# Two small vectors made in the prologue, and attention's last window inverted ahead of its predecessor's division

## The chip, the cores and the metric

The kernel runs on one core of one Trainium2 chip. The metric is the device time of one execution in microseconds (us), the median of several runs. A profile is one further execution, recorded by the hardware profiler. The engines of the core appear in it as PE (TensorE, the matrix multiplications), PEld (its weight loads), DVE (VectorE), ACT (ScalarE), POOL (GpSimd) and SP (SyncE, which issues most DMA transfers).

## The reference

Two layers work on an image batch `x` of shape (2, 56, 56, 384), all in fp32. Cut to what is computed:

```python
# layer 0: neighbourhood attention (12 heads of 32, 7x7 keys), then an MLP
q, k, v = split(layer_norm(x) @ w_qkv + b_qkv)
attn = softmax(q * 32**-0.5 @ k_nb + rpb)          # 49 neighbours of each position
x = x + (attn @ v_nb) @ w_proj + b_proj
x = x + gelu(layer_norm(x) @ w1 + b1) @ w2 + b2
# layer 1: convolution with four decaying scans, then an MLP
p = layer_norm(x) @ w_in + b_in                    # 384 -> 768
local = depthwise_conv3x3(p)
mixed = 0.25 * (lr + rl + tb + bt)(local) + local  # scans along rows and columns
mixed = layer_norm(mixed) * on_g + on_b
x = x + mixed @ w_out + b_out                      # 768 -> 384
x = x + gelu(layer_norm(x) @ w1 + b1) @ w2 + b2
```

The norm ahead of `w_out` is folded into the weights by the kernel. It needs two sums over the 768 rows of `w_out`: one weighted with `on_b`, which is added to the bias, and one weighted with `on_g / 768`, which is taken off every row. The two vectors of weights, side by side, are the tile `pair`.

## The kernel before, in words

**Order of work.** Each engine runs its own list of instructions in the order in which the kernel issues them; semaphores hold an instruction back until what it needs is there. The order is written out by hand. The stages are: a prologue (to about 50 us), attention (to about 661 us), the MLP of layer 0 over groups of 512 tokens with `w_in` of layer 1 behind it and the convolution beside it, and the MLP of layer 1.

**Prologue.** The constants go into a pool `const` first: `zeros` (line 191), `ident`, `chan` (all per-channel vectors, among them `on_g` and `on_b`, fetched by one DMA). The first group of tokens is normalised on VectorE and turned on TensorE. Then VectorE makes `bq` (line 691), the scaled bias of the queries, and takes the statistics of the second group (line 218).

**Attention.** The image is cut into 56 windows of 8x14 queries. For each window TensorE makes scores (line 539), VectorE adds the position bias (L550), ScalarE exponentiates (L560), and TensorE sums values (L579) and denominators (L590). Iteration `t` of a loop works on one part of the stream; a window is finished in three steps, which VectorE and GpSimd share:

- `gather` (L500, L505): VectorE transposes the sums into `turned`, and GpSimd copies one column of it into `totals`;
- `invert` (L509, L513 twice, L515): VectorE takes the reciprocal and checks that the totals are within bounds, and GpSimd spreads the reciprocals over `wide`;
- `divide` (L519, L522): VectorE transposes `wide` into `rec_t` and multiplies the attention output `og` by it.

`wide` has one buffer, and `turned` and `rec_t` share one. In iteration `t`, the window gathered in the iteration before is inverted at the top, and divided near the end. After the last part, `t == NS`, only the gathering of the last window is left; its inversion is at the top of `t == NS + 1`. TensorE then projects the last tokens (L609), which GpSimd prepares by adding the residual to the bias (L603).

**MLP with convolution beside it.** A group's MLP has 12 hidden blocks of 128 channels (`hidden`: three matmuls on L1185 and a GELU on ScalarE, L1196), then four products with `w2` (L1203), evicted by VectorE into the sum with the input (L1846), with statistics (L218, L219) after each. Products alternate between two PSUM banks, `y` and `y_end`. A planner, `Beside`, puts the convolution's steps on VectorE between these: taps (L1281), scans (L1228, L1232) and their sum (L1297). It deals out steps by fixed costs while the kernel is built.

**The sums of `w_out`.** In the fifth group of layer 0, a generator `prepare_w_out` is advanced once ahead of each hidden block. Its first step makes `pair` on VectorE (L1131, L1132) and takes the bank `y_end`; each of the next six issues one matmul (L1136) with a slice of `pair` as the stationary operand; then VectorE copies the two sums (L1142), they go through DRAM to all partitions (L1143, L1145), and `w_out` is rewritten (L1150, L1152). On TensorE the order is: three matmuls of block 0, L1136, three of block 1, L1136, and so on.

## Time and profile before

| what | value |
|---|---|
| median of 3 runs (lowest, highest) | 2602.36 us (2600.61, 2603.96) |
| the profiled execution's own time | 2603.72 us |
| its span, first to last instruction | 2601.9 us |
| PE busy | 2571.9 us, 99% |
| DVE busy | 1963.4 us, 75% |
| ACT busy | 982.2 us, 38% |
| POOL busy | 466.7 us, 18% |
| mean granted clock of TensorE | 0.997 |
| `pair` (L1131, L1132), one each | 0.164 and 0.161 us, at 912.6 us |
| `rec` (L509) x56, median | 0.218 us |
| `rec_t` (L519) x56, median | 0.571 us |
| `wide` on POOL (L515) x56, median | 0.534 us |

Busy time is the time in which an engine worked on an instruction, not a measure of how well. The list of waits says for each engine what it stood idle for, in total, how often and how long at most; the releaser is inferred from the semaphores. Timelines give the start from the beginning of the span and the duration; neighbouring instructions of one line are merged (xN), and a bracket shows idle time before them with its releaser. Each fp32 matmul of the program leaves two records. In the table by stretch, the columns are the length, the busy time of PE, PEld, DVE, ACT and POOL with the number of instructions, the granted clock of TensorE (1.00 is full speed), the busy share of the DMA engines, and GB/s.

### The profile page before, as it was taken

How to read it: one execution, taken by the hardware profiler on the slowest of the kernel's cores; microseconds unless marked ns; L12 is line 12 of the kernel's file. 1: busy time of each engine (PE TensorE's matmuls, PEld its weight loads, DVE VectorE, ACT ScalarE, POOL GpSimd, SP SyncE). 2: the span in 40 equal slices, each digit the busy share in tenths (PEclk: the TensorE clock that was granted, in tenths of full speed). 3: DMA queues.
4: the chain of work that ended last, by engine and by line, in shares of the span. 5: the costliest groups of instructions: out<-in, count | busy, mean ns of one | idle time of the engine just before them, and what ended most of it. 6: DMA issues, size and time to landing. Idle time of an engine off the chain costs nothing. (4 is left out here: it accounts for less than half of the span.)

```text
span 2601.9 us, 39993 instructions
## 1 busy us (share of the span) xinstructions
PE 2571.9 (99%) x16146; PEld 1643.9 (63%) x16148; DVE 1963.4 (75%) x3481; ACT 982.2 (38%) x1748; POOL 466.7 (18%) x457
## 2 busy tenths in 40 slices
PE   9999999999999999999999999999999999999999
PEld 5666666666798545555445555555555557888888
DVE  4888878887344378688998889889988836888871
ACT  5655555654443232223344423212233312333222
POOL 0111212111652000000010000000010042444342
PEclk9999999999999999999999999999999999999999
DMA  7423454225301232233346534533254331111000
GB/s 229 153 83 100 156 193 141 84 95 191 115 31 37 71 115 84 96 119 108 122 151 231 206 112 175 183 121 124 98 213 178 134 103 46 49 49 49 22 13 18
DMA packets 131652, 299.17 MB, mean 115 GB/s; under 512 B 10390, under 2 KB 85760, under 8 KB 129152
## 3 DMA queue, kind: packets, MB, share of 16 engines
q1 hardware_dynamic: 126512, 269.76, 29.9%
q10 hardware_dynamic: 4944, 26.74, 3.0%
q8 instruction: 129, 2.11, 0.3%
q14 instruction: 67, 0.55, 0.1%
HBM read 180.86 MB, written 115.61 MB: 114 GB/s over the span
## 5 line engine op out<-in xcount | busy, mean ns | idle before, releaser
L1185 PE MATMUL mm<-hT,w 128*128 128x512 f32 x1080 | 474.5, 594 | 0.1
L1281 DVE SCALAR_TENSOR_TENSOR loc<-pt,taps,loc 128x990 f32<-128x990 f32 (+9 forms) x336 | 377.2, 1123 | 11.3 <-ACT loc L1263 2.9
L1185 PEld LDWEIGHTS mm<-hT,w 128*128 128x128 f32 x1080 | 202.2, 190 | 240.2 <-issue 233.2
L226 POOL TENSOR_TENSOR rs<-rs,mhalf 128x4 f32<-128x4 f32 (+4 forms) x72 | 89.4, 1242 | 1276.7 <-DVE rs L223 1268.2
L1196 ACT ACTIVATE hid<-mm,chan 128x512 f32<-128x512 f32 x180 | 123.2, 685 | 414.1 <-PE mm L1185 414.1
L1203 PE MATMUL y<-w,hid 128*128 128x384 f32 x792 | 260.9, 486 | 0.0
L1203 PE MATMUL y_end<-w,hid 128*128 128x384 f32 x792 | 260.8, 486 | 0.0
L550 DVE TENSOR_TENSOR pts<-sc,bias 119x448 f32<-119x448 f32 (+5 forms) x396 | 219.3, 616 | 45.7 <-PE sc L539 45.3
L560 ACT ACTIVATE pts<-pts 119x448 f32<-119x448 f32 (+5 forms) x396 | 210.8, 572 | 111.1 <-DVE pts L550 106.1
L1203 PEld LDWEIGHTS y_end<-w,hid 128*128 128x128 f32 x792 | 149.9, 190 | 102.8
L1203 PEld LDWEIGHTS y<-w,hid 128*128 128x128 f32 x792 | 149.8, 190 | 102.8 <-issue 0.5
L393 PE MATMUL ps<-hT,wqkv 128*128 128x448 f32 x504 | 204.8, 550 | 2.1 <-ACT vs L438 1.5
L1185 PE MATMUL mm<-hT,w_in 128*128 128x512 f32 x396 | 172.0, 593 | 1.5 <-DVE hid_u L1571 0.9
L393 PEld LDWEIGHTS ps<-hT,wqkv 128*128 128x128 f32 x504 | 91.3, 189 | 84.4 <-issue 74.2
L1185 PEld LDWEIGHTS mm<-hT,w_in 128*128 128x128 f32 x396 | 75.0, 190 | 96.2 <-issue 91.9
L1168 DVE STREAM_TRANSPOSE hT<-xn 32x96 f32<-32x96 f32 x464 | 124.9, 269 | 11.6 <-ACT xn L244 5.6
L244 ACT ACTIVATE xn<-xc,sh,rs 128x384 f32<-128x384 f32 x98 | 64.4, 699 | 168.6 <-DVE sh L237 168.5
L1414 DVE STREAM_TRANSPOSE turned<-mx 32x192 f32<-32x192 f32 x336 | 123.9, 369 | 4.4
L579 PE MATMUL o<-pts,vt 100*32 100x112 f32 (+3 forms) x3168 | 117.1, 265 | 2.0 <-ACT pts L560 2.0
L539 PEld LDWEIGHTS sc<-qT,kT 32*100 32x100 f32 (+3 forms) x3168 | 87.8, 169 | 46.3 <-DVE sum L569 7.6
L539 PE MATMUL sc<-qT,kT 32*100 32x112 f32 (+3 forms) x3168 | 106.5, 268 | 3.1 <-DVE pts L550 3.1
L609 PE MATMUL ps<-wproj,og 128*128 128x384 f32 x294 | 105.7, 499 | 2.8 <-DVE og L522 2.2
(180 smaller groups left out, 4142.8 us busy)
## 6 DMA issues: line engine op xcount, KB each, us to landing
loc<-loc_d SPq DMA_DIRECT2D x24, 784.0 KB
mixed<-mix_d SPq DMA_DIRECT2D x24, 784.0 KB
mix_d<-mixed SPq DMA_DIRECT2D x24, 784.0 KB
xa<-x_d SPq DMA_DIRECT2D x24, 768.0 KB
bias<-in_bias_t ACTq DMA_DIRECT2D x13, 1344.0 KB
p_d<-mx SPq DMA_DIRECT2D x11, 1536.0 KB
mx<-mix_d SPq DMA_DIRECT2D x11, 1536.0 KB
pt<-p_d SPq DMA_DIRECT2D x18, 560.0 KB
```

Of the source, the lines that this page charges most:

```text
L393: nc.tensor.matmul(ps, lhsT=wqkv[:, c, m * P : (m + 1) * P], rhs=hT[:, c, half_of(n)], start=c == 0, stop=c == NC - 1,)
L539: nc.tensor.matmul(sc[i // 2][: w.keys, i % 2, q : q + TT], lhsT=kT[d, hg, w.keys_at + r * w.kc : w.keys_at + (r + w.rows) * w.kc], rhs=qT ...
L550: nc.vector.tensor_tensor(self.pts[:n, h : h + 2, lo:hi, :], sc[half][:n, :, at * TT : (at + hi - lo) * TT].rearrange("p h (c q) -> p h c ...
L560: nc.scalar.activation(t, t, AF.Exp)
L579: nc.tensor.matmul(o[i * HD : (i + 1) * HD, self.slot, :TT], lhsT=w.vt[:n, c, h * HD : (h + 1) * HD], rhs=self.pts[:n, i, c, :], start=c = ...
L609: nc.tensor.matmul(ps, lhsT=ogs[t // 7][:, c, at : at + P], rhs=wproj[:, c, :], start=c == 0, stop=c == NC - 1,)
L1168: nc.vector.transpose(hT[j : j + HD, :, k * P + i : k * P + i + HD], xn[i : i + HD, k, :].rearrange("p (c q) -> p c q", c=NC)[:, :, j : j ...
L1185: nc.tensor.matmul(ps[:, : n * P], lhsT=w[:, c, m * P : (m + 1) * P], rhs=hT[:, c, : n * P], start=c == 0, stop=c == NC - 1,)
L1196: nc.scalar.activation(t[:, : n * P], ps[:, : n * P], AF.Gelu, bias=col(b1, m))
L1203: nc.tensor.matmul(ps, lhsT=t[:, k * P : (k + 1) * P], rhs=w[:, m, :], start=m == 0, stop=m == len(lhs) - 1,)
L1281: nc.vector.scalar_tensor_tensor(to, pt[:, lo + dy - self.top : hi + dy - self.top, xt : xt + n], self.tap(dy, dx), to, ALU.mult, ALU.add,)
L1414: nc.vector.transpose(t[j : j + HD].rearrange("p (m c) -> p m c", m=NI)[:, :, i : i + HD], mx[i : i + HD, :, k * P + j : k * P + j + HD],)
```

## The change

There are two edits. `pair` moves from the MLP's pool into `const`, and is filled in the prologue, just before `bq`, by two multiplications with a number (one of them 1.0, where a copy was); the two instructions at the start of `prepare_w_out` go. The generator's steps stay as many, and L1136 reads the same values. And the last window is inverted in iteration `NS`, right after it was gathered and ahead of its predecessor's division, instead of at the top of `NS + 1`; the predecessor itself is still inverted at the top of `NS`.

```diff
     zeros = const.tile([P, MT], mybir.dt.bfloat16, name="zeros")
     nc.vector.memset(zeros, 0.0)
+    pair = const.tile([P, NI, 2], F32, name="pair")
     ident = const.tile([P, P], F32, name="ident")
...
         take_x(0, c, tps[c])
+    for i, (name, scale) in enumerate((("L1_conv_on_b", 1.0), ("L1_conv_on_g", 1.0 / INNER))):
+        nc.vector.tensor_scalar_mul(pair[:, :, i], chan[:, COL[name] : COL[name] + NI], scale)
     nc.vector.tensor_scalar_mul(bq, chan[:, COL["b_qk"] : COL["b_qk"] + NC], HD ** -0.5)
...
         store_all("v")
-        if gathered is not None:
+        if gathered is not None and t <= NS:
             gathered.invert()
         inverted, gathered = gathered, None
...
             if hi == units[s].m:
                 units[s].gathered()
+        if t == NS and gathered is not None:
+            gathered.invert()
         if inverted is not None:
             inverted.divide()
...
-            pair = wp.tile([P, NI, 2], F32, name="pair")
-            on = chan[:, COL["L1_conv_on_b"] : COL["L1_conv_on_b"] + NI]
-            og = chan[:, COL["L1_conv_on_g"] : COL["L1_conv_on_g"] + NI]
-            nc.vector.tensor_copy(pair[:, :, 0], on)
-            nc.vector.tensor_scalar_mul(pair[:, :, 1], og, 1.0 / INNER)
             ps = bank()
```

## The prediction

> **What bounds the kernel now.** I read the page first: engine shares and the clock row.

> ```profile
> PE 2571.9 (99%) x16146; PEld 1643.9 (63%) x16148; DVE 1963.4 (75%) x3481; ACT 982.2 (38%) x1748; POOL 466.7 (18%) x457
> ...
> PEclk9999999999999999999999999999999999999999
> ```

> TensorE (PE) is busy for 2571.9 of 2601.9 us, so only its 30 us of idle time, or time at a lower clock, can be saved by edits that remove no matmul. The list of waits of PE, longest first in total, says which idle time the edits touch:

> ```profile
> PE y_end L1136 <- DVE pair L1132: 4.1, 1, 4.1
> ...
> PE ps L609 <- DVE og L522: 2.2, 1, 2.2
> ```

> The first is one wait of 4.1 us, the longest of all, and it is for `pair`; the second is one wait of 2.2 us for attention's last division. Both edits therefore aim at something that TensorE really waits for. Next the timeline around the first (start us, us, engine, line, what):

> ```profile
> 899.74 6.66 DVE L1281 SCALAR_TENSOR_TENSOR loc<-pt,taps,loc 128x1045 f32<-128x1045 f32 x5
> 905.99 2.74 PE L1185 MATMUL mm<-hT,w 128*128 128x512 f32 x6
> 910.21 2.37 DVE L1232 TENSOR_TENSOR_SCAN both<-decay,both 128x1064 f32<-128x1064 f32 x1
> 912.56 0.16 DVE L1131 COPY pair<-chan 128x6 f32<-128x6 f32 x1
> 912.63 0.16 DVE L1132 TENSOR_SCALAR pair<-chan 128x6 f32<-128x6 f32 x1
> 912.84 1.44 PE L1136 MATMUL y_end<-w_out,pair 128*2 128x384 f32 x2 [4.11 <-DVE pair L1132]
> 914.22 3.73 PE L1185 MATMUL mm<-hT,w 128*128 128x512 f32 x6
> 917.88 0.81 PE L1136 MATMUL y_end<-w_out,pair 128*2 128x384 f32 x2
> 918.62 2.84 PE L1185 MATMUL mm<-hT,w 128*128 128x512 f32 x6
> 921.39 0.81 PE L1136 MATMUL y_end<-w_out,pair 128*2 128x384 f32 x2
> ```

> VectorE (DVE) runs a band of the convolution without a pause from 899.74 on, so the two tiny `pair` instructions, which need nothing but constants, come to their turn at 912.56. TensorE finished the first hidden block (L1185) at 908.73 and waits. The first L1136 and the next L1185 are also longer than their successors (1.44 and 3.73 us against 0.81 and 2.84). The busy time by stretch explains it; the column after POOL is the granted clock:

> ```profile
> 909.00:913.00 4.00, 0.16 (x1) 0.09 (x2) 3.93 (x7) 1.52 (x2) 0.28 (x1) 0.95 0.95 339
> 913.00:915.00 2.00, 2.00 (x3) 0.50 (x2) 1.09 (x3) 0.00 (x0) 1.83 (x1) 0.50 0.12 47
> 915.00:918.00 3.00, 3.00 (x7) 0.99 (x6) 2.93 (x4) 0.01 (x1) 0.00 (x0) 0.83 0.37 150
> ```

> After the pause the clock is 0.50, then 0.83 on average: the stall is paid a second time. Last, the timeline at the end of attention:

> ```profile
> 657.92 0.58 DVE L519 STREAM_TRANSPOSE rec_t<-wide 128x384 f32<-128x384 f32 x1 [0.29 <-POOL totals L505]
> 658.60 0.51 DVE L522 TENSOR_TENSOR og<-og,rec_t 128x336 f32<-128x336 f32 x1
> 659.02 0.22 DVE L509 RECIPROCAL rec<-totals 128x12 f32<-128x12 f32 x1
> 659.38 0.51 POOL L515 COPY wide<-rec 128x384 f32<-128x384 f32 x1 [1.49 <-DVE good L513]
> 659.92 0.58 DVE L519 STREAM_TRANSPOSE rec_t<-wide 128x384 f32<-128x384 f32 x1 [0.44 <-POOL wide L515]
> 661.26 0.59 PE L609 MATMUL ps<-wproj,og 128*128 128x384 f32 x1 [2.15 <-DVE og L522]
> ```

> The last window's reciprocal (L509) stands behind its predecessor's division (L519, L522), and TensorE waits for the end of that row.

> [...]

> **The change part by part.** Without the wait, TensorE keeps the rhythm of the later blocks: L1185 to L1136 takes 921.39-918.62 = 2.77, L1136 to L1185 0.74, a period of 3.51 us. From 905.99 the first L1136 would start at 908.76 and the second at 905.99+2.77+3.51 = 912.27, not at 917.88. That is 5.61 us: 4.08 of pause and 1.53 of slow clock (912.84 to 917.88 is 5.04, against 3.51).

> L1136 then waits only for `w_out`'s transfer, issued at 671, and for its bank `y_end`, which VectorE evicted at 898.45 to 899.01. Does something else stop the faster TensorE? ScalarE needs the shift of the norm (L237, until 915.02, unmoved) ahead of its GELU of the third block; that block ends at 905.99+2.74+2*3.51 = 915.75, so the GELU is not late, and there are three banks. VectorE's copy of the sums (L1142) waited 4.5 us for the last L1136 and now finds it done (932.72-5.61 = 927.1) when VectorE gets there, at 928.27: VectorE wins about 4.5 us as well, so the lines queued behind it (the L1120 and the next scan) and the sums' DMAs behind L1143 on SP's queue move along. The difference of 1.1 us is absorbed at the next evictions, where VectorE waits for TensorE; list of VectorE's waits from 933 to 1100:

> ```profile
> DVE xc L1846 <- PE y L1203: 27.2, 4, 16.2
> ```

> From 933 to the end TensorE waits 3.4 us in all (1.6 for L1440, 1.2 for xsums, 0.6 for hT), and each of those producers is itself paced by TensorE or by VectorE. So I keep the whole 5.61. The two removed instructions hold VectorE for 0.07 us each (912.56, 912.63, 912.70): nothing on the path.

> In the prologue two instructions of that kind, also some 0.07 us apart, go in front of `bq` at 8.46. `bq` is first read at 28.99, and VectorE idles 8.12 us before its next instruction (16.75), which waits for a transfer. Cost 0. If that cover were gone it would be 0.15 us. They wait for `chan`, which had landed by 5.80.

> The division: no instruction is added, the reciprocal and the two checks (L509, L513 twice) go in front of L519 and L522 of the predecessor. Reciprocal at 657.92 instead of 659.02; the checks follow at 0.14, the predecessor's L519 another 0.23 later (the spacing at 646.35 to 646.58), at 658.29, ending at 658.87. `wide` has one buffer, so GpSimd's copy may overwrite it only then, not right after the reciprocal: 658.92 to 659.01, against 659.38. Its 0.51 us now run beside the predecessor's L522 (658.97 to 659.48). The last L519 writes the buffer that this L522 reads, so it starts at about 659.58 with the 0.10 us seen from 658.50 to 658.60, against 659.92: 0.34 us, passed on to TensorE at 661.26 and to GpSimd's queue behind the copy (four L603, the norm's L226, the w1 sums), which moves as a whole. Ends: 0 (the order of waits eats it) to 0.5. I take 0.35.

> Sum: 5.61+0.35+0 = 5.96. The profiled execution took 2603.72 us (its span and 1.8 around it) and would take 2597.8; it stood 1.36 over the median of 2602.36. Forecast: 2602.36-5.96 = 2596.4 us, 0.23% less. About 0.2%, 5.2 us, is what a measurement of this kernel can tell from no change, so this forecast lies barely past it.

> **The rivals.** *The pause alone is won.* [...] the trace is one execution; where a typical one pays less at half rate, the gain is 4.08+0.35 = 4.4, giving 2598.0, no change by the bound. For it: one window at 0.50 is all that I have. [...]

> *The wait moves.* The GELU behind L237, the sums' bank or a DMA stops TensorE after all, and a part of the 5.61, 3 us or more, is lost again: 2599.4 to 2602.4. Against it are the margins above, of which ScalarE's, 0.7 us on the GELU and then three banks, is the smallest.

> *The division does nothing*: `wide`'s one buffer holds the copy back until no time is won; 2596.7, inside the main case.

> *Slower.* `pair` now lies in the constants' pool ahead of all attention tiles, which in the built program start 64 bytes later. [...] Priced: 0.2 us in each of attention's 56 windows is 11.2 us, 2602.4-6.0+11.2 = 2607.6; from 0.106 us a window the gain is gone, from 0.2 the kernel is slower beyond the bound. For it: ScalarE, TensorE's feeder, waits for transfers 7.8 us in all between 60 and 661 us, GpSimd 10.1. Against: those are waits for a store's end and for `xr`, none of TensorE's, ScalarE's or VectorE's is for `vt`, which is asked for two windows (some 22 us) ahead, and the DMA engines are 0.39 to 0.44 busy there.

> **How the numbers follow.** Whole gain 0.68 (own range 2594.2 to 2597.6, nine tenths of it past the bound); pause alone 0.16 (a small part past the bound); the wait moves 0.09; slower 0.07. Faster: 0.61+0.02 = 0.63; slower 0.07; the rest, 0.30, within 0.2%. The range leaves out the slower case, most of the moved wait and a tail below: 2593.8 to 2600.2.

> **What would show it.** Right: the wait of L1136 for `pair` is gone from the list; L1136 follows the first L1185 block at once, blocks 3.5 us apart from the first on; the clock is 1.00 from 905 to 920; L1142 no longer waits 4.5 us; L609 waits about 1.8 us instead of 2.15; the copy to `wide` starts right after the predecessor's L519. Wrong: a new wait of TensorE of over 1 us between 905 and 1100, L1136 held by a transfer, or a changed mean of L550 or L560.

## The result and the profile after

| what | before | after |
|---|---|---|
| median, 22 runs of each beside one another (lowest, highest) | 2602.72 us (2598.81, 2607.53) | 2598.77 us (2593.85, 2603.30) |
| ratio to before, 95% interval | | 0.9985 [0.9978, 0.9991] |
| the profiled execution's own time | 2603.72 us | 2598.40 us |
| its span | 2601.9 us | 2596.6 us |
| mean granted clock of TensorE | 0.997 | 0.998 |

The changed kernel takes 3.95 us less (1.5 parts in a thousand; from the interval, 2.3 to 5.7 us). The forecast was 5.96 us less. The time lies in the range, and the sign is right, but by the bound of 0.2% this measurement says "no change" where the likeliest case said "faster". A second measurement of the same kernel, in another set of runs (below), gave 0.9971 [0.9961, 0.9981], that is 7.25 us less by the medians. The forecast ratio, 0.9977, lies between the two.

Lines after 192 stand one line lower in the changed kernel, up to the new loop at 692 (L509 is L510, L522 is L523, L609 is L610); L1136, L1142 and L1185 have kept their numbers. First the page of the changed kernel, engine shares and clock row:

```profile
PE 2570.7 (99%) x16146; PEld 1644.1 (63%) x16148; DVE 1964.2 (76%) x3481; ACT 982.9 (38%) x1748; POOL 467.0 (18%) x457
...
PEclk9999999999999999999999999999999999999999
```

TensorE's busy time is 1.2 us smaller, though it does the same matmuls, which fits less time at half rate (before, the clock was 0.50 from 912.62 to 916.04 us; around the same work it is 1.00 now). The rest of the 5.3 us between the two spans, 4.1 us, is idle time. The waits of PE in the changed kernel, longest first in total (total us, times, longest):

```profile
PE sc L540 <- DVE pts L551: 3.5, 7, 0.7
PE ps L610 <- DVE og L523: 2.1, 1, 2.1
```

The wait for `pair`, 4.1 us and first in the list before, is gone. The wait for the last division is not: 2.12 us, against 2.15. Next the timeline around the first L1136 of the changed kernel (start us, us, engine, line, what):

```profile
906.84 2.74 PE L1185 MATMUL mm<-hT,w 128*128 128x512 f32 x6
909.51 0.81 PE L1136 MATMUL y_end<-w_out,pair 128*2 128x384 f32 x2
910.25 2.84 PE L1185 MATMUL mm<-hT,w 128*128 128x512 f32 x6
913.02 0.81 PE L1136 MATMUL y_end<-w_out,pair 128*2 128x384 f32 x2
...
915.84 0.71 ACT L245 ACTIVATE xn<-xc,sh,rs 128x384 f32<-128x384 f32 x1 [2.03 <-DVE sh L238]
...
928.96 0.54 DVE L1142 COPY sums<-y_end 2x384 f32<-2x384 f32 x1
```

The rhythm is that of the forecast from the first block on: L1136 starts 2.67 us after the block, the next one 3.51 us later, and both take 0.81 us. L1142 has no wait in front of it, where VectorE stood idle for 4.49 us before. ScalarE waits 2.03 us for the shift of the norm, until 915.84, while TensorE works through its third block and the next L1136 (916.53 in the same timeline) without a stop. The busy time by stretch (length, PE, PEld, DVE, ACT, POOL, clock, DMA share, GB/s), changed kernel:

```profile
909.00:913.00 4.00, 4.00 (x10) 1.14 (x8) 3.93 (x3) 1.76 (x2) 0.00 (x0) 1.00 1.02 339
913.00:915.00 2.00, 2.00 (x6) 0.76 (x6) 1.74 (x3) 0.69 (x1) 1.43 (x1) 1.00 0.26 105
```

TensorE is busy throughout, at the full clock. The last view is the end of attention in the changed kernel:

```profile
658.97 0.23 DVE L510 RECIPROCAL rec<-totals 128x12 f32<-128x12 f32 x1 [0.30 <-POOL totals L506]
659.35 0.57 DVE L520 STREAM_TRANSPOSE rec_t<-wide 128x384 f32<-128x384 f32 x1
660.02 0.51 DVE L523 TENSOR_TENSOR og<-og,rec_t 128x336 f32<-128x336 f32 x1
660.05 0.85 POOL L516 COPY wide<-rec 128x384 f32<-128x384 f32 x1 [1.11 <-DVE rec_t L520]
660.93 0.58 DVE L520 STREAM_TRANSPOSE rec_t<-wide 128x384 f32<-128x384 f32 x1 [0.40 <-POOL wide L516]
662.27 8.01 PE L610 MATMUL ps<-wproj,og 128*128 128x384 f32 x24 [2.12 <-DVE og L523]
```

The order is the new one: the reciprocal in front of the predecessor's L520, the copy to `wide` as soon as that L520 has read it. But the copy takes 0.85 us, not the 0.51 it took before, and from the end of the copy of `totals` (658.93) to L610 it is 3.34 us, against 3.37 before.

### The profile page after: what moved, and what is told of

The parts are those of the page before. It is cut to its first block, busy times and chain, and to the rows that moved or that the text cites. A ratio compares the mean times of both kernels' runs of the same rounds, so it can differ in the third digit from the quotient of the medians.

```text
span 2596.6 us, 39994 instructions
## 1 busy us (share of the span) xinstructions
PE 2570.7 (99%) x16146; PEld 1644.1 (63%) x16148; DVE 1964.2 (76%) x3481; ACT 982.9 (38%) x1748; POOL 467.0 (18%) x457
## 5 line engine op out<-in xcount | busy, mean ns | idle before, releaser
L1185 PE MATMUL mm<-hT,w 128*128 128x512 f32 x1080 | 473.6, 593 | 0.1
L1281 DVE SCALAR_TENSOR_TENSOR loc<-pt,taps,loc 128x990 f32<-128x990 f32 (+9 forms) x336 | 377.2, 1123 | 10.2 <-ACT loc L1263 1.9
L1185 PEld LDWEIGHTS mm<-hT,w 128*128 128x128 f32 x1080 | 201.8, 190 | 239.0 <-issue 231.4
L1203 PE MATMUL y<-w,hid 128*128 128x384 f32 x792 | 260.9, 486 | 0.0
L1203 PE MATMUL y_end<-w,hid 128*128 128x384 f32 x792 | 260.8, 486 | 0.0
L1203 PEld LDWEIGHTS y_end<-w,hid 128*128 128x128 f32 x792 | 149.9, 190 | 102.8
L1203 PEld LDWEIGHTS y<-w,hid 128*128 128x128 f32 x792 | 149.8, 190 | 102.8 <-issue 0.5
L1185 PE MATMUL mm<-hT,w_in 128*128 128x512 f32 x396 | 172.0, 593 | 1.5 <-DVE hid_u L1571 0.9
L1185 PEld LDWEIGHTS mm<-hT,w_in 128*128 128x128 f32 x396 | 75.0, 190 | 96.2 <-issue 91.9
L245 ACT ACTIVATE xn<-xc,sh,rs 128x384 f32<-128x384 f32 x98 | 64.4, 699 | 170.2 <-DVE sh L238 170.1
L610 PE MATMUL ps<-wproj,og 128*128 128x384 f32 x294 | 106.4, 501 | 2.8 <-DVE og L523 2.1
```

What stands on the lines that cost most here:

```text
L610: nc.tensor.matmul(ps, lhsT=ogs[t // 7][:, c, at : at + P], rhs=wproj[:, c, :], start=c == 0, stop=c == NC - 1,)
L1185: nc.tensor.matmul(ps[:, : n * P], lhsT=w[:, c, m * P : (m + 1) * P], rhs=hT[:, c, : n * P], start=c == 0, stop=c == NC - 1,)
L1203: nc.tensor.matmul(ps, lhsT=t[:, k * P : (k + 1) * P], rhs=w[:, m, :], start=m == 0, stop=m == len(lhs) - 1,)
L1281: nc.vector.scalar_tensor_tensor(to, pt[:, lo + dy - self.top : hi + dy - self.top, xt : xt + n], self.tap(dy, dx), to, ALU.mult, ALU.add,)
```

## The experiments

All ratios are to the kernel before, run beside the experiments on the same chip; there were three such sets, on three chips. A ratio is the one on record, and differs from the quotient of the two medians by up to 0.0009 (the medians of no_pair_again give 0.9973). A kernel's median scatters by several microseconds, so the traces are read by parts as well. This table has, for the profiled execution of each kernel, how long after the first hidden block of the fifth group the first L1136 starts, how long that block lies ahead of the end of the span, and the time from the end of the last copy to `totals` to the projection that waits for it. It is made from the timelines; all in us.

| kernel | ratio [95%] | block to first L1136 | block to end | totals to projection |
|---|---|---|---|---|
| before | 1 | 6.85 | 1695.93 | 3.37 |
| division_only | 1.0008 [1.0000, 1.0017] | 6.85 | 1697.13 | 3.33 |
| shifted_64 | 1.0002 [0.9993, 1.0010] | 6.85 | 1695.42 | 3.38 |
| pair_gpsimd | 1.0012 [1.0005, 1.0018] | 9.17 | 1697.69 | 3.38 |
| after (first measurement) | 0.9985 [0.9978, 0.9991] | 2.67 | 1689.76 | 3.34 |
| changed_again | 0.9971 [0.9961, 0.9981] | 2.67 | 1689.90 | 3.34 |
| pair_only | 0.9984 [0.9975, 0.9993] | 2.67 | 1690.03 | 3.38 |
| no_pair | 0.9962 [0.9949, 0.9975] | 2.67 | 1689.47 | 3.38 |
| no_pair_again | 0.9964 [0.9953, 0.9976] | 2.67 | 1689.75 | 3.38 |
| no_pair_shifted | 0.9968 [0.9956, 0.9979] | 2.67 | 1689.54 | 3.37 |
| no_pair_divide_first | 0.9965 [0.9952, 0.9978] | 2.67 | 1689.43 | 2.24 |
| wide_twice | one execution | 2.67 | 1689.66 | 3.54 |
| six_ready_pairs | 0.9997 [0.9987, 1.0007] | 2.67 | 1695.71 | 3.34 |
| six_late_pairs | 1.0161 [1.0145, 1.0176] | 2.67 | 1739.46 | 3.34 |

**The two edits apart.** One kernel has only the new `pair`, the other only the earlier inversion.

```diff
 # pair_only: the changed kernel with these two edits undone
-        if gathered is not None and t <= NS:
+        if gathered is not None:
...
-        if t == NS and gathered is not None:
-            gathered.invert()
 # division_only: the kernel before with these two edits made
-        if gathered is not None:
+        if gathered is not None and t <= NS:
...
+        if t == NS and gathered is not None:
+            gathered.invert()
```

> The two vectors made in the prologue, the division as it was. Whole gain (the pause and the slow clock behind it): 5.6 us less than before, a ratio of 0.9978. Pause alone: 4.1 us less, 0.9984. Shifted addresses (the 64 bytes cost some 1.5 us that the faster MLP hides): about 4 us less, and then the run that makes the vectors on GpSimd, where nothing is shifted, wins 1.5 us more than this one. In the trace, the first L1136 follows the first hidden block at once in all three.

> The last window inverted ahead of its predecessor's division, the pair as before. My working: 0.35 us less. From the trace of the changed kernel: 0.05 us or nothing, because GpSimd's copy to wide takes 0.85 us there instead of 0.51 while VectorE multiplies beside it. Neither can be told from 1.000 by the times; the trace decides, by the time from the end of the copy of the totals to TensorE's first L609, 3.38 us before: 3.03 by the working, 3.3 by the changed trace.

Measured: 2598.00 us (0.9984) and 2603.98 us (1.0008), beside 2602.62 before. The pair alone gives the whole change; the division gives nothing, 0.04 us in its own stretch of the trace (3.33 against 3.37). Even the 0.35 us of the forecast would be too small to be seen in a median; the trace decides it. That division_only came out a little slower goes with its clock: its 13 executions had a mean clock of 0.9966, the 55 of the kernel before 0.9975 (what that is worth is worked out below). The trace of division_only showed something else, in the busy time by stretch around the pause that it still has (columns as above):

```profile
913.00:916.00 3.00, 0.40 (x1) 0.09 (x2) 3.00 (x5) 0.28 (x1) 0.53 (x1) 0.83 0.85 329
916.00:919.00 3.00, 3.00 (x5) 1.00 (x4) 2.06 (x4) 0.00 (x0) 1.59 (x1) 0.50 0.44 182
919.00:922.00 3.00, 3.00 (x5) 0.85 (x3) 2.96 (x3) 0.00 (x0) 0.00 (x0) 0.54 0.00 0
```

The pause of L1136 is the same, 4.1 us, but the clock stays at half rate for 6.83 us (914.95 to 921.78), where it was 3.41 us (912.62 to 916.04) before. So the price of one and the same pause differs by its place. The time from the first to the sixth L1136 says how much: 17.54 us in the changed kernel, 19.07 before, 19.19 in shifted_64, 20.55 in division_only; the half rate cost 1.5, 1.65 and 3.0 us.

**The addresses.** The rival that ended slower was a shift of attention's tiles by 64 bytes. This kernel makes that shift and nothing else:

```diff
-    mhalf = const.tile([P, NT], F32, name="mhalf")
-    nc.vector.memset(mhalf, -0.5)
+    mhalf = const.tile([P, NT + 16], F32, name="mhalf")
+    nc.vector.memset(mhalf[:, :NT], -0.5)
```

> The kernel before with one constant tile 64 bytes longer: no instruction changes, every attention tile lies 64 bytes further on, as in the changed kernel. If the addresses do not matter: 1.000. If they are what took 1.5 to 2 us of the forecast gain: 1.0006 to 1.0008, with longer vt and xr transfers or a longer mean of L550, L560 or L579 in the trace.

Measured: 2603.07 us, 1.0002 [0.9993, 1.0010]. The shift costs at most a thousandth by this interval; the rival asked for 4 in a thousand. The smaller cost that the expectation also names, 0.6 to 0.8 in a thousand, is not excluded by it.

**The pair on another engine.** If L1136 waits only because `pair` stands in VectorE's queue behind the convolution, then GpSimd can make it in time.

```diff
-            nc.vector.tensor_copy(pair[:, :, 0], on)
-            nc.vector.tensor_scalar_mul(pair[:, :, 1], og, 1.0 / INNER)
+            nc.gpsimd.tensor_copy(pair[:, :, 0], on)
+            nc.gpsimd.tensor_scalar_mul(pair[:, :, 1], og, 1.0 / INNER)
```

> The pair made at its old place in the MLP, by GpSimd, which has been idle for 50 us there, and not by VectorE; no address and no other instruction moves. Whole gain: 5.6 us less, 0.9978. Pause alone: 4.1 us, 0.9984. Shifted addresses: 5.6 us here, and less in the run with the pair in the prologue. Wait for VectorE in another shape (GpSimd held up by VectorE): the pause remains, and 1.000.

Measured: 2605.44 us, 1.0012 [1.0005, 1.0018]; slower, against the expectation. Its timeline tells why:

```profile
912.11 0.14 DVE L223 SCALAR_TENSOR_TENSOR rs<-mv,ones 128x4 f32<-128x4 f32 x1
912.32 2.04 POOL L226 TENSOR_TENSOR rs<-rs,mhalf 128x4 f32<-128x4 f32 x1 [56.86 <-DVE rs L223]
914.48 0.24 POOL L1132 TENSOR_SCALAR pair<-chan 128x6 f32<-128x6 f32 x1
914.77 1.44 PE L1136 MATMUL y_end<-w_out,pair 128*2 128x384 f32 x2 [6.43 <-POOL pair L1132]
```

GpSimd had been idle for 56.86 us, but the next instruction of its queue was the norm's L226, which waits for VectorE's L223, and VectorE reaches that only after the convolution's band. `pair` stood behind it: the pause of TensorE became 6.43 us. An engine that is idle is not an engine that is free; what stands at the head of its queue decides. As a test of dose the miss is of use: a pause 2.3 us longer made the kernel slower by 2.8 us in the median (2605.44 against 2602.62) and by 1.8 us from the block to the end.

**No pair at all.** The sums can be taken with `on_b` and `on_g` as they lie side by side in `chan`, and the division by 768 made where the sums are copied. The bias then takes back the factor.

```diff
-            nc.vector.tensor_copy(t[:2, 2 * C : 3 * C], ps[:2, :])
+            nc.vector.tensor_scalar_mul(t[:2, 2 * C : 3 * C], ps[:2, :], 1.0 / INNER)
...
+            at = COL["L1_conv_on_g"]
+            pair = chan[:, at : at + 2 * NI].rearrange("p (i c) -> p c i", i=2)
...
-            nc.vector.tensor_tensor(row("b_out"), t[:, :C], row("b_out"), ALU.add)
+            nc.vector.scalar_tensor_tensor(
+                row("b_out"), t[:, C : 2 * C], float(INNER), row("b_out"), ALU.mult, ALU.add
+            )
```

(The rewriting of `w_out` reads `t[:, :C]` instead of the second half, since `on_g` comes first; the pair of the prologue and the division's edits are left out.)

> No pair at all: L1136 reads the columns of on_g and on_b where they lie in chan, and the factor 1/768 is applied when the sums are copied. No instruction in the prologue, no address moved, the division as before. If the 64 bytes cost some 1.5 us in attention: 5.6 to 6 us less than before, 0.9977 to 0.9978, more than the run with the pair in the prologue (0.9984). If they cost nothing: the same as that run. In both, the blocks follow each other at once, and from the fifth group's first block to the end it is 1690 us, against 1696 before.

Measured: 2594.08 us beside 2602.76 before, 0.9962 [0.9949, 0.9975]. The gain is there without any new tile and without the prologue's two instructions. It looked larger than the changed kernel's (0.9985), which would speak for a cost of the tile in `const`; the pairs of runs further below are there to decide that.

**The price of one pause.** To enlarge the disputed size, six further groups issue one more product (its result is unused), once with a stationary operand that VectorE has to copy at that moment, as `pair` was, and once with `pair` itself, which is ready.

```diff
+    pair_2 = const.tile([P, NI, 2], F32, name="pair_2")
...
+        def late_pair():
+            nc.vector.tensor_copy(pair_2[:, :, 0], pair[:, :, 0])
+            nc.vector.tensor_copy(pair_2[:, :, 1], pair[:, :, 1])
+            ps = bank()
+            yield
+            nc.tensor.matmul(
+                ps[:2, :], lhsT=pair_2[:, 0, :], rhs=w_out[:, 0, :], start=True, stop=True
+            )
...
+            if EARLY.stop + 1 < g < EARLY.stop + 8:
+                preparing = late_pair()
```

(`six_ready_pairs` leaves out the two copies and multiplies with `pair[:, 0, :]`.)

> The changed kernel, with a late pair in each of six later groups: two tiny copies on VectorE at the group's start, where the pair was made before, and one more matmul of the L1136 kind that waits for them, its product unused. From the changed trace those copies come 3.6 to 5.4 us after the first block's end, 27.6 us for the six. To be read against the run with the same six matmuls and no late copies. Pause alone: about 28 us more than that run. Pause and slow clock: 37 to 43 us more (1.5 to 2.5 us for each of the six).

> The changed kernel with the same six extra matmuls, which read the pair of the prologue and wait for nothing; their product is unused. Both theories: 6 times 0.74 us, 4.4 us more than the changed kernel, so about the time of the kernel before, 0.9998 to 1.0005; no pause in the trace.

Measured: 2645.75 and 2603.09 us, 42.66 us apart (43.75 from the first block to the end in the traces). The six products alone add 5.95 us in the trace (1695.71 against 1689.76), which is why six_ready_pairs stands where the kernel before does. That is 0.99 us each, where 0.74 was expected; both kernels have them, so the comparison does not rest on it. The waits of PE in `six_late_pairs`, longest first, begin with the new ones, six in two banks:

```profile
PE y L1165 <- DVE pair L1162: 15.0, 3, 5.6
PE y_end L1165 <- DVE pair L1162: 13.7, 3, 5.2
```

These are 28.7 us of pauses, 4.8 on average. The remaining 14 to 15 us are no wait of TensorE. One of the six stretches (columns as above) shows where they are:

```profile
995.00:1010.00 15.00, 10.29 (x18) 4.03 (x19) 13.75 (x22) 2.56 (x4) 3.28 (x2) 0.77 0.16 64
```

TensorE is busy for 10.29 of 15 us, but the mean clock is 0.77. So a pause of 4.8 us costs on average another 2.3 to 2.5 us at half rate (14 to 15 us over six). Half of the time that each stood at half rate outside its pause gives 1.7 us for one of the six and 2.7 to 2.9 for the others. "The pause alone is won" is refuted: the clock fell at every one of the six.

**The predecessor divided earlier.** In iteration `NS` VectorE idles ahead of the last gathering. Here the predecessor is divided there, so that only the last window's inversion and division stand behind the gathering; `pair` is that of no_pair.

```diff
+        if t == NS and inverted is not None:
+            inverted.divide()
...
             if hi == units[s].m:
                 units[s].gathered()
+        if t == NS and gathered is not None:
+            gathered.invert()
         if inverted is not None:
-            inverted.divide()
+            if t != NS:
+                inverted.divide()
```

> No pair, and in attention's last round the predecessor is divided ahead of the gathering of the last window, when VectorE is idle for 1.1 us, so that nothing stands between the last totals and their inversion and GpSimd's copy has no VectorE instruction beside it. From the copy of the totals to L609: 3.38 us before, 3.34 with the changed order; 2.2 if the copy takes 0.51 us again, 2.6 if it stays at 0.85. In time 0.8 to 1.2 us under the run without a pair, which can hardly be told; against before 0.9973 to 0.9981.

The timeline of that kernel at the end of attention:

```profile
655.40 0.51 DVE L522 TENSOR_TENSOR og<-og,rec_t 128x336 f32<-128x336 f32 x1
...
657.18 0.54 POOL L515 COPY wide<-rec 128x384 f32<-128x384 f32 x1 [0.33 <-DVE good L513]
...
659.10 8.01 PE L609 MATMUL ps<-wproj,og 128*128 128x384 f32 x24 [1.08 <-DVE og L522]
```

The predecessor's L522 is done before the copy begins, the copy takes 0.54 us, and TensorE waits 1.08 us instead of 2.15; from `totals` to the projection it is 2.24 us instead of 3.37. This is the 1.1 us that lay in the division. In the median, 2595.13 against no_pair's 2594.08, it can't be seen (0.9965 against 0.9962, with intervals of about a thousandth either way).

**Addresses again, on one chip.** no_pair with the 64-byte shift, no_pair and the changed kernel once more beside each other, and one execution with a second buffer for `wide`:

```diff
 # no_pair_shifted: no_pair with
-    mhalf = const.tile([P, NT], F32, name="mhalf")
-    nc.vector.memset(mhalf, -0.5)
+    mhalf = const.tile([P, NT + 16], F32, name="mhalf")
+    nc.vector.memset(mhalf[:, :NT], -0.5)
 # wide_twice: the changed kernel with
-            self.wide = lp.tile([P, BLOCKS, HD], F32, name="wide")
+            self.wide = lp.tile([P, BLOCKS, HD], F32, name="wide", bufs=2)
```

> The run without a pair, with one constant tile 64 bytes longer: no instruction changes, and attention's tiles lie where they lie in the changed kernel. If the 64 bytes are what took 2 to 5 us of the gain: 0.9978 to 0.9985, and in the trace a wait of TensorE of about 1.5 us near 385 us, behind ScalarE, behind a store of values. If they cost nothing: the time of the run without a pair, repeated here on the same chip.

> The run without a pair once more, beside the other three. From six late pairs (4.8 us of pause and 2.3 us of slow clock each) the pause of 4.1 us should be worth about 6.4 us: 0.9975. The first measurement was 0.9962 with an end of its interval at 0.9975. If addresses are without effect, the changed kernel beside it has the same ratio.

> The changed kernel once more, beside the run without a pair. If the addresses cost: 0.9983 to 0.9987, 2 us or more over that run. If not: both alike, at some 0.9975 to 0.998.

> The changed kernel with two buffers for wide, so that GpSimd's copy need not wait for the predecessor's L519. From the end of the totals' copy to L609: 3.34 us in the changed kernel. If the one buffer is what eats the division's gain: the copy starts 0.3 us behind the totals and the last L519 stands right behind the predecessor's multiplication, about 2.7 us, unless the copy is slowed to 0.85 us or more by VectorE beside it, which would still leave it done before then. If the order on VectorE is what counts: 3.3.

Measured beside 2603.10 before: 2595.25 (0.9968), 2596.12 (0.9964) and 2595.85 us (0.9971). The three intervals overlap almost wholly. The shift costs nothing that can be seen, with the pair in `chan` as without that edit, and on one chip no cost of the tile in `const` can be seen either, with intervals of about a thousandth either way: most of what looked like one after no_pair was the difference between two sets of runs.

The second buffer was to let the copy to `wide` start right after the checks, and it does. Timeline of wide_twice:

```profile
659.83 0.54 POOL L516 COPY wide<-rec 128x384 f32<-128x384 f32 x1 [0.33 <-DVE good L514]
...
660.34 4.46 POOL L604 TENSOR_TENSOR xr<-xr,shift 128x384 f32<-128x384 f32 x4
660.59 1.10 DVE L523 TENSOR_TENSOR og<-og,rec_t 128x336 f32<-128x336 f32 x1
```

The copy is back at 0.54 us. But GpSimd is free earlier, too, and begins with L604; the predecessor's L523, whose turn is then, takes 1.10 us instead of 0.51. From `totals` to the projection it is 3.54 us, more than before.

**Where the scatter comes from.** The time from the start to the end of the last copy to `totals` lies ahead of both edits' effect, save for the two instructions of the prologue (wide_twice and no_pair_divide_first change attention before it, too). Over the fourteen traces it varies from 654.9 to 661.7 us: 657.9 before, 658.9 after, 661.7 in pair_only, 655.1 in no_pair_shifted. From the sixth L1136 to the end all but the two with six products more lie within 1669.2 to 1670.0. In the stretch from 630 to 670 us the mean clock was 0.87 before and in pair_only, and 0.96 in no_pair_shifted. So single executions differ by up to 7 us in attention, and the clock falls there at different places.

The clock of the unprofiled executions is on record too, to a thousandth. Over the 231 executions that have it, an execution's time moves within one kernel and chip by 2.4 us for each thousandth of its mean clock (correlation -0.85); a thousandth of 2600 us is 2.6. So the larger part of the scatter goes with the clock. For division_only above, 0.0009 is worth 2.1 us, which covers its difference. Of the 3.3 us between the two measurements of the change, 2.9 lie in the changed kernel's median (2598.77 and 2595.85); its mean clock was 0.9980 and 0.9986, which is worth about 1.5 us. The rest stays open.

## Why the prediction was right, and where it was not

**The pause: right.** The step "Without the wait, TensorE keeps the rhythm of the later blocks" holds to a tenth of a microsecond: first L1136 2.67 us after the block (2.77 was said, from the spacing of a later block), period 3.51 us. The first L1136 comes 4.18 us earlier after its block; 4.08 was said.

**The slow clock: right in kind, too small.** The term was 1.53 us, from the one execution that I had. Three executions with the same pause show 1.5, 1.65 and 3.0 us, and the six pauses of six_late_pairs 2.3 to 2.5 on average. From the block to the end, kernels with the 4.1 us pause take 1696.16 us on average (three traces), those without it and without additions 1689.69 (eight traces): 6.47 us, where the sum said 5.61. Less the 4.18 us of the pause, the term is thus 2.3 us rather than 1.5; 2.05 of it lie between the first and the sixth L1136, and the other 0.2 us is no more than the scatter behind that. I gave the likelier error the wrong sign: the rival said that a typical execution pays less than the one shown, and the runs show that it pays as much or more. The forecast used the doubt about its one execution only downwards for this pause. After the other pause, the 2.15 us at 661, the clock stayed at 1.00 in the trace before; in five of the fourteen traces it fell within 1.1 us after the end of that wait.

**Kept to the end: right.** From the sixth L1136 to the end 1670.0 us before and 1669.55 after: nothing is given back. VectorE's L1142 no longer waits, and ScalarE's margin sufficed, though its L245 came to wait 2.03 us. The rival "the wait moves" has no place in the trace: TensorE has no wait between 905 and 1100 us in the changed kernel.

**The prologue: right as far as it can be seen.** Kernels with the two instructions there and without them have overlapping intervals on one chip (0.9971 and 0.9964), and their medians are 0.3 us apart, with the smaller one on the side of the kernel that has them.

**The division: wrong.** The order became the one forecast, up to the start of the copy. The step that failed is "Its 0.51 us now run beside the predecessor's L522": beside it the copy takes 0.85 us, and 0.34 us, the whole gain, is gone. 0.04 us is left. I had the overlap in my hands and priced both instructions as if alone. The traces give the amount, for VectorE's product of `og` beside GpSimd's copy to `wide` or its sum of `xr` and `shift`: the later one of the two takes longer by what is left of the earlier one when it starts, less 0.14 us. Why, they do not show. The copy starts with 0.48 us of L523 left and takes 0.85 us instead of 0.51, in all five traces in which it starts beside L523. VectorE's L523 starts in wide_twice with 0.73 us of the first L604 left and takes 1.10 us instead of 0.51. Of the 784 multiplications of `og` in the fourteen traces, 49 take over 0.52 us; every one of them starts while GpSimd adds `shift` to `xr` (L603, L604), and every one fits this amount to 0.01 us. no_pair_divide_first, where they don't meet, wins 1.1 us.

The trace before held this price already, in the middle of attention:

```profile
297.05 1.12 POOL L603 TENSOR_TENSOR xr<-xr,shift 128x384 f32<-128x384 f32 x1 [2.85 <-DMA xr<-in_x]
297.84 0.70 DVE L522 TENSOR_TENSOR og<-og,rec_t 128x336 f32<-128x336 f32 x1
```

Here 0.33 us of L603 is left at 297.84, and L522 takes 0.19 us longer than its 0.51. In the working, the copy at 659.01 would have met 0.47 us of an L522 that ends at 659.48: 0.33 us longer, and the gain of 0.34 us would have been put at nothing.

**Slower by addresses: refuted at the size that was priced**, twice (1.0002; 0.9968 against 0.9964). The cost of 11.2 us, 0.2 us in each window of attention, was a supposition of mine with no trace behind it, and is in no run here.

**The whole.** Locally the forecast of 5.96 us became 6.47 plus 0.04, an error of half a microsecond. The first measurement shows 3.95 us (2.3 to 5.7), so that by it the likeliest case, past the 0.2%, did not come about, and the second one does show it. A gain as large as the bound is a coin's throw for a single measurement; a chance of 0.61 for "past the bound" out of 0.68 for the whole gain was too sure. Why the two measurements differ by 3.3 us is known for about half of it, the clock; whether chip or chance made the rest stays open.

## What to carry to other kernels

A tiny operand for TensorE belongs ahead of the stage that uses it, or out of the program: price its lateness as the pause plus the half-rate time after it (here 1.5 to 3.1 us, on average 2.35, in ten pauses of 3.8 to 6.4 us), and remember that moving it to an idle engine helps only if the head of that engine's queue isn't waiting itself (here the pause grew from 4.11 to 6.43 us). When an edit brings two engines' instructions side by side that ran one after the other, don't price both as if alone; look in the trace for a place where the same two already meet, and whether the later one lengthens there. And an edit's gain is best read from a stretch of the trace that begins just ahead of it, when the stages before scatter by more than it is worth.

## What the runs showed of the hardware

The same pause of 4.11 us was followed by 3.41 us at clock 0.50 in two executions and by 6.83 us in a third. Busy time by stretch (columns as above), cut where the clock changed; the first two lines are of the kernel before, the other three of division_only:

```profile
909.21:912.62 3.41, 0.00 (x0) 0.00 (x0) 3.34 (x5) 1.31 (x2) 0.00 (x0) 1.00 1.03 371
912.62:916.04 3.42, 3.20 (x4) 0.93 (x5) 2.51 (x6) 0.00 (x0) 2.11 (x1) 0.50 0.41 167
911.54:914.95 3.41, 0.00 (x0) 0.00 (x0) 3.34 (x3) 1.75 (x2) 0.00 (x0) 1.00 0.97 341
914.95:918.37 3.42, 2.77 (x4) 0.93 (x5) 2.51 (x7) 0.00 (x0) 2.11 (x1) 0.50 0.40 162
918.37:921.78 3.41, 3.41 (x5) 1.01 (x3) 3.34 (x4) 0.00 (x0) 0.00 (x0) 0.50 0.14 59
```

The clock also fell after windows that were not idle: at 632.73 us in the kernel before, after one in which TensorE was busy for 1.66 of the 3.41 us. It fell 40 times within the fourteen traces, their first and last windows apart: after all 20 full-rate windows in which TensorE was busy for less than 0.414 of the time, after 20 of the 40 with a share from there to 0.617, and after none of the 10498 with more. Twenty-seven of the 40 falls lie in attention, near 385 us and from 631 to 666 us, where TensorE is busy for such shares. Where they lie differs from one trace to the next: from 630 to 670 us the mean clock was 0.87 before and 0.96 in no_pair_shifted, and the last copy to `totals` ended at 657.9 and 655.1 us.

What the two engines take longer beside each other moved with their order rather than vanish: one more buffer took 0.31 us from GpSimd's copy and put 0.59 us on VectorE's product.
